# Another order for the first phase of a block-sparse gate kernel, with 21 instead of 13 opening matmuls that nobody reads

## The chip, the cores and the metric

The kernel runs on one core of one Trainium2 chip. The time is the device time of one execution, in microseconds (us). The core's engines run side by side, each through its own list of instructions in order: TensorE (PE, with its weight loads PEld), VectorE (DVE), ScalarE (ACT), GpSimd (POOL), and SyncE (SP), which here issues most DMA transfers.

## The reference, cut to what matters

```python
xn = _layernorm(x, axis=-1)                                   # x is [2, 1024, 1024], f32
bm = mask.reshape(Nb, 32, Kb, 32).sum(axis=(1, 3)) > 0        # 32 x 32 blocks
w = (weight.reshape(Nb, 32, Kb, 32) * bm[:, None, :, None]).reshape(N, K)
s = einsum('bsk,nk->bsn', xn, w) + bias
q = einsum('bi,ki->bk', xn.mean(axis=1), Wq)
coeffs = softmax(einsum('bk,ek->be', q, lora_keys) / sqrt(128))
base = einsum('bsi,oi->bso', xn, W_org)
delta = einsum('be,bser,ero->bso', coeffs, einsum('bsi,eir->bser', xn, lora_down), lora_up)
out = x + s * silu(base + delta)
```

All of it is float32. The change touches only batch 0, the product s for the first 512 output columns, and the way to the coefficients.

## The kernel before, in words

Every operand of a product is kept as two parts in the reduced format float32r: hi, the rounded value, which ACT writes with a copy, and lo, what remains, which DVE (at a few places POOL) writes with a subtraction. One 128-row step of a product is three matmuls in one accumulator: hi by hi (L457), hi by lo (L460), lo by hi (L461). So each step needs the hi and lo of its piece of x (tile g0, "xgrp" in the trace) and of its piece of the masked weights (s0, "slot").

The first phase makes s for the 1024 rows of batch 0 and the first 512 columns. Rows come in tiles 0 to 7 of 128. For tiles 0 to 3 the columns are done in two quarters of 256: p0 to p3 (their steps are called by t0 to t3) and q0 to q3 (by u0 to u3). Tiles 4 to 7 do 512 columns at once (q4 to q7, by u4 to u7). t0(0, 4) means steps 0 to 3 of the eight. The accumulators share four PSUM buffers in the order in which they are opened (open_gemm); one is taken again when its result has been moved out (quarter_evac, tile_evac on DVE). The first buffer is for warm_up(n): n matmuls of 512 columns on ones, whose result nobody reads.

The row tiles 0 to 3 arrive untransposed. For each, x_stats (DVE, two halves), rstd_of (two small DVE operations and a power on POOL), shift_of (DVE) and x_norm_half (ACT, twice) normalise it; x_turn (four PE transposes per half, into one of two pairs of PSUM buffers) turns it; x_hi (ACT) and x_lo (DVE) split it. Tiles 4 to 7 are read transposed already (xprep: a DMA of xT into one of six buffers "xt", a subtraction of the means on DVE, the hi copy on ACT; xprep_lo). spread_means makes their row of means with four transposes on PE. The tiles are also normalised in rows and added up into acc (add_acc, 1024 columns each), from which halves, query, scores and soft make the coefficients; scale_up multiplies lora_up with them for the product that follows the phase, y_mul.

The mask: mask_sum sums 0/1 blocks (DVE or ACT), mask_spread and mask_apply_mm (eight small bf16 matmuls, L276) spread the block flags over the partitions into the PSUM tile mp, mask_apply_cp copies it to m_sb. w_mul multiplies weights with it, from mp on DVE and from m_sb on POOL, which does not read PSUM here; w_hi and w_lo split them, for a quarter q and rows k0 on.

The order on PE, DVE, ACT and POOL is the order in which the program calls these helpers, since the block is under manual_schedule with those four engines; the order of SP's transfers is chosen by the scheduler of the language. A queue never overtakes: an instruction that waits holds all behind it on its engine.

Of the kernel before, what the change touches and what calls it, by code (L numbers as in the profile page):

```python
# [22 lines left out]
NH = 512  # L23
# [1 line left out]
TPB = S // P  # L25
E_, R_, KQ = 8, 64, 128
EPS = 1e-5
NWARM = 13
NWARM2 = 12


@with_exitstack
def kernel(
# [118 lines left out]
    def rstd_of(t):  # L152

        mv = small.tile([P, 2], F32, name="mv", bufs=10)
        nc.vector.bn_aggr(mv, stat[t])
        ve = small.tile([P, 1], F32, name="ve", bufs=3)
        nc.vector.tensor_scalar(ve, mv[:, 1:2], EPS, None, ALU.add)
        nc.gpsimd.tensor_tensor(rstd[:, t : t + 1], ve, mhalf, ALU.pow)
        means[t] = mv[:, 0:1]

    def shift_of(t):

        mr = small.tile([P, 1], F32, name="mr", bufs=3)
        nc.vector.tensor_scalar(mr, means[t], rstd[:, t : t + 1], -1.0, ALU.mult, ALU.mult)
        stat[t] = mr
# [84 lines left out]
    def mask_sum(qr, c, mt, eng, part=0):  # L250

        if qr not in msum:
            msum[qr] = small.tile([P, 2, 2], F32, name="s2")
        o = msum[qr][:, part, c : c + 1]
        if eng is nc.scalar:
            nc.scalar.activation(mt.bitcast(F32), mt, AF.Copy, accum_out=o)
        else:
            nc.vector.tensor_reduce(o, mt, AX.X, ALU.add)  # L258
# [23 lines left out]
    def mask_apply_cp(qr, k0=0, k1=NKT, copy=nc.vector.tensor_copy):  # L282
        copy(m_sb[:, k0:k1, 8 * qr : 8 * (qr + 1)], spread[qr][:, k0:k1, :])
# [300 lines left out]
    def w_mul(q, k0, eng, n=2):  # L584

        v = wh[q][:, k0 : k0 + n, :].rearrange("p k (b i) -> p k b i", i=32)
        m = m_sb[:, k0 : k0 + n, 8 * q : 8 * (q + 1)] if eng is nc.gpsimd else spread[q][:, k0 : k0 + n, :]
        eng.tensor_tensor(v, v, m.unsqueeze(3).to_broadcast([P, n, 8, 32]), ALU.mult)
# [10 lines left out]
    def x_turn(i, h):  # L599
        turn((i, h), lambda k: xr[i][:, (4 * h + k) * P : (4 * h + k + 1) * P])  # L600

    def x_hi(i, h):
        nc.scalar.copy(g0[:, 4 * h : 4 * h + 4, 0, i * P : (i + 1) * P], turned[(i, h)])
# [7 lines left out]
    def x_stats(i, h):  # L611
        bn(i, xr[i], h)
# [31 lines left out]
    def x_norm_half(i, h):  # L644
        v = xr[i][:, h * NH : (h + 1) * NH]
        norm(i, v, v)
# [5 lines left out]
    with tc.manual_schedule(engines={mybir.EngineType.PE, mybir.EngineType.DVE, mybir.EngineType.Activation, mybir.EngineType.Pool}):  # L652
# [19 lines left out]
        def warm_up(n):  # L672
            for _ in range(n):
                nc.tensor.matmul(
                    warm, lhsT=ones_r, rhs=ones_r.unsqueeze(1).to_broadcast([P, 4, P]), start=True, stop=True
                )

        warm_up(NWARM)
        x_stats(0, 0)
        x_stats(0, 1)  # L680
        rstd_of(0)
# [1 line left out]
        x_norm_half(0, 0)  # L683
        x_norm_half(0, 1)
        x_turn(0, 0)
        x_turn(0, 1)
        warm_up(NWARM2)
        x_stats(1, 0)
        x_stats(1, 1)
        rstd_of(1)  # L690
        mask_sum(0, 0, mh[0][:, 0, :], nc.vector)
        x_hi(0, 0)
        mask_sum(0, 1, mh[0][:, 1, NH:], nc.scalar, 1)
        mask_sum(0, 1, mh[0][:, 1, :NH], nc.vector)
        mask_join(0)
        mask_spread(0)
        shift_of(1)
        mask_apply_mm(0)
        warm_up(4)
        x_hi(0, 1)  # L700
        mask_apply_cp(0, 0, 4, nc.scalar.copy)
        w_mul(0, 0, nc.vector, 1)
        w_mul(0, 1, nc.vector, 1)
        w_mul(0, 2, nc.gpsimd)
        w_hi(0, 0, 1)
        w_hi(0, 1, 1)
        x_lo(0, 0)
        x_norm_half(1, 0)
        w_hi(0, 2)
        w_lo(0, 0, nc.vector, 1)  # L710
        w_lo(0, 1, nc.vector, 1)
        p0, t0 = open_gemm(0, 0, s0, 0, NQ)
        p1, t1 = open_gemm(0, 1, s0, 0, NQ)

        keep_busy = lambda kt: warm_up((4, 1, 2, 0)[kt])
        t0(0, 1, keep_busy)
        x_turn(1, 0)
        t0(1, 2, keep_busy)
        x_hi(1, 0)
        mask_apply_cp(0, 4, 8, nc.scalar.copy)  # L720
        w_lo(0, 2)
        t0(2, 4, keep_busy)
        x_lo(1, 0)
        w_mul(0, 4, nc.vector)
        w_mul(0, 6, nc.gpsimd)
        x_norm_half(1, 1)
        w_hi(0, 4)
        t1(0, 3)
        x_turn(1, 1)
        x_lo(0, 1)  # L730
        w_hi(0, 6)
        w_lo(0, 4)
        x_hi(1, 1)
        t1(3, 4)
        t0(4, 6)
        w_lo(0, 6, nc.gpsimd)
        x_stats(2, 0)
        x_stats(2, 1)
        rstd_of(2)
        mask_sum(1, 0, mh[1][:, 0, :], nc.scalar)  # L740
        t0(6, 8)
        x_lo(1, 1)
        shift_of(2)
        x_norm_half(2, 0)
        x_norm_half(2, 1)
        x_stats(3, 0)
        x_stats(3, 1)
        rstd_of(3)
        add_acc(1, nc.gpsimd)
        t1(4, 7)  # L750
        x_turn(2, 0)
        t1(7, 8)
        x_hi(2, 0)
        x_turn(2, 1)
        x_lo(2, 0)
        shift_of(3)
        x_hi(2, 1)
        x_norm_half(3, 0)
        x_norm_half(3, 1)
        x_lo(2, 1)  # L760
        mask_sum(1, 1, mh[1][:, 1, :], nc.vector)
        mask_spread(1)
        p2, t2 = open_gemm(0, 2, s0, 0, NQ)
        t2(0, 4)
        x_turn(3, 0)
        x_hi(3, 0)
        t2(4, 5)
        mask_apply_mm(1)
        mask_apply_cp(1, copy=nc.scalar.copy)
        w_mul(1, 4, nc.gpsimd)  # L770
        w_mul(1, 6, nc.gpsimd)
        x_lo(3, 0)
        x_turn(3, 1)
        t2(5, 8)
        w_mul(1, 0, nc.vector)
        x_hi(3, 1)
        x_lo(3, 1)
        w_hi(1, 0)
        w_mul(1, 2, nc.vector)
        p3, t3 = open_gemm(0, 3, s0, 0, NQ)  # L780
        t3(0, 8)
        w_hi(1, 2)
        w_hi(1, 4)
        w_hi(1, 6)
        w_lo(1, 0)
        quarter_evac(0, 0, p0)
        w_lo(1, 2)
        mean_sum(6)
        mean_sum(7)
        w_lo(1, 4)  # L790
        w_lo(1, 6)
        quarter_evac(1, 0, p1)
        x_stats(4, 0)
        x_stats(4, 1)
        x_stats(5, 0)
        rstd_of(4)
        x_stats(5, 1)
        q0, u0 = open_gemm(0, 0, s0, NQ, NQ)
        u0(0, 8)
        shift_of(4)  # L800
        x_norm(4)
        rstd_of(5)
        mean_of(6)
        mean_of(7)
        q1, u1 = open_gemm(0, 1, s0, NQ, NQ)
        u1(0, 6)
        spread_means(0, 1)
        u1(6, 8)
        quarter_evac(2, 0, p2)
        xprep(0, 1, 0)  # L810
        xprep(0, 1, 1)
        shift_of(5)
        x_norm(5)
        xprep_lo(0, 1, 0)
        quarter_evac(3, 0, p3)
        q2, u2 = open_gemm(0, 2, s0, NQ, NQ)
        u2(0, 8)
        q3, u3 = open_gemm(0, 3, s0, NQ, NQ)
        u3(0, 8)
        for kt in range(2, 6):  # L820
            xprep(0, 1, kt)
            xprep_lo(0, 1, kt - 1, nc.gpsimd if kt == 4 else nc.vector)
            if kt == 3:
                quarter_evac(0, 1, q0)
            square_sum(6 + (kt - 2) // 2, kt % 2)
        xprep(0, 1, 6)
        xprep_lo(0, 1, 5, nc.gpsimd)
        xprep(0, 1, 7)
        rstd_from(6)
        rstd_from(7)  # L830
        xprep_lo(0, 1, 6)
        xprep_lo(0, 1, 7)
        quarter_evac(1, 1, q1)
        q4, u4 = open_gemm(0, 4, s0)
        u4(0, 8)
        shift_of(6)
        shift_of(7)
        x_norm(6)
        x_norm(7)
        for i in range(2, 6):  # L840
            add_acc(i, nc.vector)
        quarter_evac(2, 1, q2)
        add_acc(6, nc.vector)
        quarter_evac(3, 1, q3)
        for h in range(2):
            add_acc(7, nc.vector, h)
        halves, query, scores, soft = coeffs(0)
        halves()
        y00 = new_slot()
        q5, u5 = open_gemm(0, 5, s0)  # L850
        u5(0, 8)
        q6, u6 = open_gemm(0, 6, s0)
        u6(0, 4)
        query()
        tile_evac("s", 0, 0, 4, q4)
        y_prep(0, 0, 0)
        u6(4, 7)
        scores()
        tile_evac("s", 0, 0, 5, q5)
        soft()  # L860
        scale_up(0, 0)
        y_prep(0, 0, 1)
        u6(7, 8)
        tile_evac("s", 0, 0, 6, q6)
        q7, u7 = open_gemm(0, 7, s0)
        u7(0, 8)
        for k in range(NKT):
            y_mul(0, 0, k)
            if k == 0:
                tile_evac("s", 0, 0, 7, q7)  # L870
            y_sum(0, 0, k)
            if k + 2 < NKT:
                y_prep(0, 0, k + 2)
            y_hi(y00, 0, 0, k)
            y_lo(y00, 0, 0, k)
            if k == 1:
                act_stats(0)
# [684 lines left out]
```

## Time and profile before

| | us |
|---|---|
| median of 3 runs | 438.7 (438.32 to 438.96) |
| the profiled execution | 438.7 |
| its span in the trace | 437.0 |
| first matmul without a use | 1.12 |
| first x_turn | 7.30 |
| first product (L457) | 13.15 |
| end of the first quarter of tiles 0 to 3, start of u0 | 30.68 |
| start of u4 | 42.62 |
| start of y_mul | 65.60 |
| last matmul starts | 432.58 |
| TensorE clock granted | 1.00 |

The span runs from the first instruction to the last; the 1.7 us between it and the execution's time lie outside the trace. "Busy" is the share of the span in which an engine works; a matmul without a use counts as busy. The names in the trace are those of the tiles: "pt" is a transposed tile in PSUM, "xgrp" the split x, "slot" the split weights, "ramp" the raw weights and masks, "mp" the spread mask, "acc_ps" an accumulator. A profile line can name what ended an engine's idle time, after "<-".

### The profile page before, as it was taken

What the parts mean: (1) busy time and instruction counts of PE and PEld (TensorE: products, weight loads), DVE (VectorE), ACT (ScalarE), POOL (GpSimd) and SP (SyncE); (2) the same over time, 40 slices, a digit from 0 to 9 for tenths busy, and PEclk for the clock granted to TensorE, in tenths of its full rate; (3) what the DMA queues carried; (4) which work ended last, traced back from release to release, by engine and by line L of the source; (5) the groups of instructions that cost most, each with busy time, mean ns of one, the idle gap of its engine ahead of it and who ended that gap; (6) DMA issues with size and microseconds to landing.
All of it is one profiled execution on the core that took longest, in us unless ns stands there. A gap on an engine that the chain in (4) does not pass through costs nothing.

```text
span 437.0 us, 5766 instructions
## 1 busy us (share of the span) xinstructions
PE 429.5 (98%) x2029; PEld 357.8 (82%) x2029; DVE 305.0 (70%) x508; ACT 184.6 (42%) x312; POOL 79.0 (18%) x103
## 2 busy tenths in 40 slices
PE   7999999999999999999999999999999999999996
PEld 5899888888888888888888878888888888888885
DVE  5889977766527779878957779867647385275624
ACT  3787436354731222246332454466335233441510
POOL 4342210002220323133130330010020030002000
PEclk9999999999999999999999999999999999999999
DMA  7994706787896799984689788976282165228003
GB/s 271 414 355 162 218 26 221 237 249 225 250 309 170 252 264 309 314 307 144 179 213 307 242 246 226 347 239 197 68 220 70 48 145 147 93 53 210 27 1 121
DMA packets 44477, 88.48 MB, mean 202 GB/s; under 512 B 4624, under 2 KB 13088, under 8 KB 44448
## 3 DMA queue, kind: packets, MB, share of 16 engines
q1 hardware_dynamic: 28944, 64.77, 44.3%
q0 software_dynamic: 6624, 16.26, 16.0%
q10 hardware_dynamic: 8880, 7.08, 5.1%
q8 instruction: 16, 0.26, 0.3%
q14 instruction: 13, 0.11, 0.1%
HBM read 68.17 MB, written 19.93 MB: 202 GB/s over the span
## 4 chain that ended last, share of the span: by engine, by line
PE 95%; DVE 1%; DMA 1%; ACT 1%; issue 0%; POOL 0%; SPq 0%; DVEq 0%
PE acc_ps L1393 25%; PE acc_ps L461 13%; PE acc_ps L457 13%; PE acc_ps L460 13%; PE py L1393 10%; PE psv L1148 6%; PE psw L422 3%; PE psw L423 3%; PE psw L421 3%; PE psw L1148 2%; DMA raw<-in_x_dram 1%; PE pt L211 0%; DVE s L258 0%; ACT slot L591 0%; POOL slot L595 0%
## 5 line engine op out<-in xcount | busy, mean ns | idle before, releaser
L1393 PE MATMUL acc_ps<-xw,ow 128*128 128x512 f32 (+1 forms) x492 | 111.9, 384 | 0.0
L457 PE MATMUL acc_ps<-slot,xgrp 128*128 128x512 f32 (+1 forms) x288 | 106.5, 370 | 0.2 <-ACT slot L591 0.2
L1393 PEld LDWEIGHTS acc_ps<-xw,ow 128*128 128x128 f32 x492 | 90.8, 188 | 18.3
L461 PE MATMUL acc_ps<-slot,xgrp 128*128 128x512 f32 (+1 forms) x288 | 105.5, 366 | 0.2 <-DVE xgrp L607 0.2
L460 PE MATMUL acc_ps<-slot,xgrp 128*128 128x512 f32 (+1 forms) x288 | 105.4, 366 | 0.1
L461 PEld LDWEIGHTS acc_ps<-slot,xgrp 128*128 128x128 f32 x288 | 54.2, 188 | 9.6 <-DVE xgrp L607 0.6
L457 PEld LDWEIGHTS acc_ps<-slot,xgrp 128*128 128x128 f32 x288 | 54.3, 188 | 9.3 <-ACT slot L591 0.6
L460 PEld LDWEIGHTS acc_ps<-slot,xgrp 128*128 128x128 f32 x288 | 54.3, 188 | 8.9 <-POOL slot L595 0.3
L1393 PE MATMUL py<-xw,ow 128*128 128x512 f32 x192 | 46.3, 389 | 0.0
L1393 PEld LDWEIGHTS py<-xw,ow 128*128 128x128 f32 x192 | 36.0, 188 | 7.5
L1262 DVE TENSOR_TENSOR ow<-raw,ow 128x1024 fp32r<-128x1024 f32 (+1 forms) x32 | 34.6, 1087 | 9.2 <-ACT ow L1261 9.1
L1261 ACT CAST ow<-raw 128x1024 fp32r<-128x1024 f32 (+1 forms) x32 | 29.5, 940 | 2.5 <-DVE raw L1255 1.7
L1376 POOL DMA_DIRECT2D gate<-in_xT_dram x12 | 10.5, 913 | 94.0 <-DVE gate L1370 67.8
L509 POOL DMA_DIRECT2D stash<-in_x_dram x16 | 14.4, 901 | 66.9 <-DVE stash L506 66.9
L431 ACT CAST slot<-wo 128x512 fp32r<-128x512 f32 x16 | 9.9, 620 | 35.8 <-DVE wo L428 35.6
L421 PE MATMUL psw<-cut,dhi 128*128 128x512 f32 x64 | 24.9, 389 | 0.0
L422 PE MATMUL psw<-cut,dhi 128*128 128x512 f32 x64 | 24.9, 389 | 0.0
L423 PE MATMUL psw<-cut,dlo 128*128 128x512 f32 x64 | 24.9, 389 | 0.0
L1437 DVE TENSOR_TENSOR py<-py,s 128x512 f32<-128x512 f32 x8 | 5.6, 698 | 26.8 <-ACT s L1400 26.8
L1255 DVE TENSOR_TENSOR raw<-raw 128x512 f32<-128x512 f32 x32 | 21.3, 688 | 0.9 <-DMA raw<-yu 0.4
L1247 DVE TENSOR_TENSOR raw<-raw,m_sb 128x1024 f32<-128x1024 f32 x8 | 9.7, 1221 | 14.4 <-DMA raw<-in_wu_dram 14.4
L506 DVE TENSOR_TENSOR stash<-stash,mine 128x512 f32<-128x512 f32 x16 | 11.1, 692 | 10.8 <-ACT mine L482 10.6
(211 smaller groups left out, 604.0 us busy)
## 6 DMA issues: line engine op xcount, KB each, us to landing
wo<-in_worgT_dram SPq DMA_DIRECT2D x24, 256.0 KB, 4.1
raw<-in_x_dram SPq DMA_DIRECT2D x11, 512.0 KB, 4.8
ds<-in_down_dram SPq DMA_DIRECT2D x16, 256.0 KB, 3.2
stash<-in_x_dram POOLq DMA_DIRECT2D x16, 256.0 KB, 5.7
raw<-in_wu_dram SPq DMA_DIRECT2D x8, 512.0 KB, 5.7
raw<-yu SPq DMA_DIRECT2D x8, 512.0 KB, 3.8
out_dram<-stash ACTq DMA_DIRECT2D x14, 256.0 KB, 4.2
misc<-xv SPq DMA_DIRECT2D x12, 256.0 KB, 4.2
```

Source lines behind the costliest of these rows:

```text
L421: nc.tensor.matmul(ps, lhsT=dhi[:, c, :], rhs=u[c][:, 0, :], start=c == 0, stop=False)
L422: nc.tensor.matmul(ps, lhsT=dhi[:, c, :], rhs=u[c][:, 1, :], start=False, stop=False)
L423: nc.tensor.matmul(ps, lhsT=dlo[:, c, :], rhs=u[c][:, 0, :], start=False, stop=c == 3)
L457: nc.tensor.matmul(ps, lhsT=xs[:, kt, 0, cols], rhs=w[:, kt, 0, wc], start=kt == 0, stop=False)
L460: nc.tensor.matmul(ps, lhsT=xs[:, kt, 0, cols], rhs=w[:, kt, 1, wc], start=False, stop=False)
L461: nc.tensor.matmul(ps, lhsT=xs[:, kt, 1, cols], rhs=w[:, kt, 0, wc], start=False, stop=kt == NKT - 1)
L509: nc.gpsimd.dma_start(res, x[at], accum_op=ALU.add)
L1148: nc.tensor.matmul(ps, lhsT=w[:, a, wl, c, :], rhs=u[:, ul, :], start=start and c == 0 and n == 0, stop=c == 1 and n == 2, skip_group_chec ...
L1255: nc.vector.tensor_tensor(raw[:, o], raw[:, a], raw[:, b], op)
L1261: nc.scalar.copy(o[:, a:b, 0], raw[:, a:b])
L1262: nc.vector.tensor_tensor(o[:, a:b, 1], raw[:, a:b], o[:, a:b, 0].bitcast(F32), ALU.subtract)
L1393: nc.tensor.matmul(ps, lhsT=o[:, a, wl, j, :], rhs=xw[j][:, m, xl, cols], start=start and j == 0 and k == 0, stop=j == 3 and k == 2, skip_ ...
```

## The change

The helpers stay as they are. The calls of the first phase come in another order, PE's, DVE's, ACT's and POOL's lists with them. No call is added or taken away but those of warm_up: 21 instead of 13 at the start, 12 as before in the second place, 5 instead of 4 after the first mask products, and in the first steps of tile 0 one behind step 0 and three behind step 2 instead of four, one and two. The diff, cut in its second half:

```diff
-NWARM = 13
-NWARM2 = 12
+NWARM = 21
...
         warm_up(NWARM)
+        keep_busy = lambda kt: warm_up((1, 0, 3, 0)[kt])
+        halves, query, scores, soft = coeffs(0)
+
+        p0, t0 = open_gemm(0, 0, s0, 0, NQ)
+        p1, t1 = open_gemm(0, 1, s0, 0, NQ)
         x_stats(0, 0)
...
         x_turn(0, 0)
+        x_hi(0, 0)
         x_turn(0, 1)
-        warm_up(NWARM2)
+        warm_up(12)
+        p2, t2 = open_gemm(0, 2, s0, 0, NQ)
         x_stats(1, 0)
         x_stats(1, 1)
         rstd_of(1)
+        x_hi(0, 1)
+        mask_sum(0, 1, mh[0][:, 1, NH:], nc.scalar, 1)
         mask_sum(0, 0, mh[0][:, 0, :], nc.vector)
-        x_hi(0, 0)
-        mask_sum(0, 1, mh[0][:, 1, NH:], nc.scalar, 1)
+        shift_of(1)
+        x_norm_half(1, 0)
+        x_norm_half(1, 1)
         mask_sum(0, 1, mh[0][:, 1, :NH], nc.vector)
         mask_join(0)
         mask_spread(0)
-        shift_of(1)
         mask_apply_mm(0)
-        warm_up(4)
-        x_hi(0, 1)
         mask_apply_cp(0, 0, 4, nc.scalar.copy)
+        x_lo(0, 0)
+        mask_apply_cp(0, 4, 8, nc.scalar.copy)
+        warm_up(5)
         w_mul(0, 0, nc.vector, 1)
+        w_hi(0, 0, 1)
         w_mul(0, 1, nc.vector, 1)
+        w_mul(0, 4, nc.vector)
+        w_hi(0, 1, 1)
+        x_turn(1, 0)
+        w_lo(0, 0, nc.vector, 1)
+        t0(0, 1, keep_busy)
+        w_lo(0, 1, nc.vector, 1)
+        x_stats(2, 0)
         w_mul(0, 2, nc.gpsimd)
...
-        p0, t0 = open_gemm(0, 0, s0, 0, NQ)
-        p1, t1 = open_gemm(0, 1, s0, 0, NQ)
-
-        keep_busy = lambda kt: warm_up((4, 1, 2, 0)[kt])
-        t0(0, 1, keep_busy)
-        x_turn(1, 0)
-        t0(1, 2, keep_busy)
         x_hi(1, 0)
-        mask_apply_cp(0, 4, 8, nc.scalar.copy)
         w_lo(0, 2)
+        w_mul(0, 6, nc.gpsimd)
+        t0(1, 2)
+        x_turn(1, 1)
+        x_stats(2, 1)
+        w_hi(0, 6)
+        w_lo(0, 6, nc.gpsimd)
         t0(2, 4, keep_busy)
+        x_hi(1, 1)
         x_lo(1, 0)
...
+        t1(0, 3)
+        t1(3, 4)
+        rstd_of(2)
         w_hi(0, 4)
+        w_lo(0, 4)
         x_lo(0, 1)
+        mask_sum(1, 0, mh[1][:, 0, :], nc.scalar)
+        q0, u0 = open_gemm(0, 0, s0, NQ, NQ)
         t0(4, 6)
         t0(6, 8)
         shift_of(2)
         x_norm_half(2, 0)
         x_norm_half(2, 1)
+        x_turn(2, 0)
+        x_hi(2, 0)
+        x_lo(1, 1)
+        t1(4, 7)
         x_stats(3, 0)
         x_stats(3, 1)
         rstd_of(3)
+        x_turn(2, 1)
+        x_hi(2, 1)
         t1(7, 8)
         x_lo(2, 0)
+        t2(0, 4)
         shift_of(3)
         x_norm_half(3, 0)
         x_norm_half(3, 1)
         mask_sum(1, 1, mh[1][:, 1, :], nc.vector)
         mask_spread(1)
         mask_apply_mm(1)
         mask_apply_cp(1, copy=nc.scalar.copy)
+        quarter_evac(0, 0, p0)
+        x_turn(3, 0)
+        x_turn(3, 1)
+        x_hi(3, 0)
+        x_lo(2, 1)
+        t2(4, 5)
+        w_mul(1, 2, nc.vector)
+        w_mul(1, 0, nc.vector)
+        x_lo(3, 0)
+        x_stats(4, 0)
+        x_hi(3, 1)
+        t2(5, 8)
...
+        w_mul(1, 6, nc.gpsimd)
+        quarter_evac(1, 0, p1)
+        w_hi(1, 2)
+        w_lo(1, 2)
+        mean_sum(7)
+        w_lo(1, 0)
+        mean_of(7)
+        x_stats(5, 0)
+        q1, u1 = open_gemm(0, 1, s0, NQ, NQ)
+        add_acc(1, nc.gpsimd)
+        w_mul(1, 4, nc.gpsimd)
+        w_hi(1, 4)
+        w_lo(1, 4)
+        w_hi(1, 6)
+        w_lo(1, 6)
+        quarter_evac(2, 0, p2)
+        u1(0, 6)
...
+        u0(0, 8)
...
         shift_of(4)
         spread_means(0, 1)
         xprep(0, 1, 0)
         xprep(0, 1, 1)
+        xprep(0, 1, 2)
+        quarter_evac(0, 1, q0)
+        u1(6, 8)
+        xprep_lo(0, 1, 1, nc.vector)
+        xprep_lo(0, 1, 0)
+        xprep(0, 1, 3)
+        xprep_lo(0, 1, 3, nc.gpsimd)
+        xprep_lo(0, 1, 2, nc.vector)
...
+        u3(0, 8)
...
+        u2(0, 8)
...
+        u6(0, 4)
...
         u4(0, 8)
+        u5(0, 8)
+        add_acc(7, nc.vector, 1)
         halves()
         query()
-        tile_evac("s", 0, 0, 4, q4)
         y_prep(0, 0, 0)
         u6(4, 7)
         scores()
-        tile_evac("s", 0, 0, 5, q5)
         soft()
-        scale_up(0, 0)
-        y_prep(0, 0, 1)
+        tile_evac("s", 0, 0, 4, q4)
         u6(7, 8)
         tile_evac("s", 0, 0, 6, q6)
         q7, u7 = open_gemm(0, 7, s0)
         u7(0, 8)
+        scale_up(0, 0)
+        y_prep(0, 0, 1)
+        tile_evac("s", 0, 0, 5, q5)
+        y00 = new_slot()
```

Between spread_means and u5 the other xprep, xprep_lo, shift_of, x_norm and add_acc calls are mixed with the evictions; add_acc runs in the order 2, 3, 5, 6, 4, 7, and the norms of tiles 4 to 7 in the order 4, 7, 5, 6. The rest of the kernel, from y_mul on, is the same.

More of the change, by code (lines that the diff above doesn't have):

```diff
@@ L696 @@
         mask_spread(0)
-        shift_of(1)
         mask_apply_mm(0)
-        warm_up(4)
-        x_hi(0, 1)
         mask_apply_cp(0, 0, 4, nc.scalar.copy)
+        x_lo(0, 0)
+        mask_apply_cp(0, 4, 8, nc.scalar.copy)
+        warm_up(5)
         w_mul(0, 0, nc.vector, 1)
+        w_hi(0, 0, 1)
         w_mul(0, 1, nc.vector, 1)
+        w_mul(0, 4, nc.vector)
[5 more added lines that the diff above has]
+        x_stats(2, 0)
         w_mul(0, 2, nc.gpsimd)
[L705 to L708, printed above, removed]
         w_hi(0, 2)
-        w_lo(0, 0, nc.vector, 1)
-        w_lo(0, 1, nc.vector, 1)
-        p0, t0 = open_gemm(0, 0, s0, 0, NQ)
-        p1, t1 = open_gemm(0, 1, s0, 0, NQ)
-        keep_busy = lambda kt: warm_up((4, 1, 2, 0)[kt])
-        t0(0, 1, keep_busy)
-        x_turn(1, 0)
-        t0(1, 2, keep_busy)
         x_hi(1, 0)
-        mask_apply_cp(0, 4, 8, nc.scalar.copy)
         w_lo(0, 2)
+        w_mul(0, 6, nc.gpsimd)
[4 more added lines that the diff above has]
+        w_lo(0, 6, nc.gpsimd)
         t0(2, 4, keep_busy)
+        x_hi(1, 1)
         x_lo(1, 0)
-        w_mul(0, 4, nc.vector)
-        w_mul(0, 6, nc.gpsimd)
-        x_norm_half(1, 1)
+        t1(0, 3)
+        t1(3, 4)
+        rstd_of(2)
         w_hi(0, 4)
-        t1(0, 3)
-        x_turn(1, 1)
+        w_lo(0, 4)
         x_lo(0, 1)
[L731 to L734, printed above, removed]
+        mask_sum(1, 0, mh[1][:, 0, :], nc.scalar)
+        q0, u0 = open_gemm(0, 0, s0, NQ, NQ)
         t0(4, 6)
[L736 to L740, printed above, removed]
         t0(6, 8)
-        x_lo(1, 1)
         shift_of(2)
@@ L748 @@
         rstd_of(3)
-        add_acc(1, nc.gpsimd)
-        t1(4, 7)
-        x_turn(2, 0)
+        x_turn(2, 1)
+        x_hi(2, 1)
         t1(7, 8)
-        x_hi(2, 0)
-        x_turn(2, 1)
         x_lo(2, 0)
+        t2(0, 4)
         shift_of(3)
-        x_hi(2, 1)
         x_norm_half(3, 0)
         x_norm_half(3, 1)
-        x_lo(2, 1)
         mask_sum(1, 1, mh[1][:, 1, :], nc.vector)
         mask_spread(1)
-        p2, t2 = open_gemm(0, 2, s0, 0, NQ)
-        t2(0, 4)
-        x_turn(3, 0)
@@ L766 @@
-        x_hi(3, 0)
-        t2(4, 5)
         mask_apply_mm(1)
         mask_apply_cp(1, copy=nc.scalar.copy)
-        w_mul(1, 4, nc.gpsimd)
[L771 to L782, printed above, removed]
+        quarter_evac(0, 0, p0)
+        x_turn(3, 0)
+        x_turn(3, 1)
@@ new lines @@
+        x_hi(3, 0)
[7 more added lines that the diff above has]
+        t2(5, 8)
+        p3, t3 = open_gemm(0, 3, s0, 0, NQ)
+        w_hi(1, 0)
+        x_lo(3, 1)
+        t3(0, 8)
+        w_mul(1, 6, nc.gpsimd)
[7 more added lines that the diff above has]
+        q1, u1 = open_gemm(0, 1, s0, NQ, NQ)
@@ L783 @@
+        add_acc(1, nc.gpsimd)
+        w_mul(1, 4, nc.gpsimd)
         w_hi(1, 4)
+        w_lo(1, 4)
         w_hi(1, 6)
-        w_lo(1, 0)
-        quarter_evac(0, 0, p0)
-        w_lo(1, 2)
+        w_lo(1, 6)
+        quarter_evac(2, 0, p2)
+        u1(0, 6)
         mean_sum(6)
[L789 to L793, printed above, removed]
+        mean_of(6)
+        square_sum(6, 0)
         x_stats(4, 1)
-        x_stats(5, 0)
+        square_sum(6, 1)
@@ L796 @@
+        quarter_evac(3, 0, p3)
         rstd_of(4)
+        square_sum(7, 0)
+        square_sum(7, 1)
+        u0(0, 8)
         x_stats(5, 1)
-        q0, u0 = open_gemm(0, 0, s0, NQ, NQ)
-        u0(0, 8)
+        rstd_of(5)
+        q3, u3 = open_gemm(0, 3, s0, NQ, NQ)
         shift_of(4)
[L801 to L806, printed above, removed]
         spread_means(0, 1)
-        u1(6, 8)
-        quarter_evac(2, 0, p2)
@@ L810 @@
         xprep(0, 1, 0)
         xprep(0, 1, 1)
-        shift_of(5)
-        x_norm(5)
[L814 to L825, printed above, removed]
@@ L826 @@
-        xprep(0, 1, 6)
-        xprep_lo(0, 1, 5, nc.gpsimd)
[L828 to L833, printed above, removed]
+        xprep(0, 1, 2)
[6 more added lines that the diff above has]
+        xprep_lo(0, 1, 2, nc.vector)
+        q2, u2 = open_gemm(0, 2, s0, NQ, NQ)
@@ new lines @@
+        q6, u6 = open_gemm(0, 6, s0)
+        u3(0, 8)
+        quarter_evac(3, 1, q3)
+        xprep(0, 1, 4)
+        shift_of(5)
+        xprep(0, 1, 5)
+        x_norm(4)
+        rstd_from(7)
+        xprep(0, 1, 6)
+        rstd_from(6)
+        quarter_evac(1, 1, q1)
+        xprep_lo(0, 1, 4, nc.vector)
+        add_acc(2, nc.vector)
+        shift_of(7)
+        q5, u5 = open_gemm(0, 5, s0)
+        x_norm(7)
+        xprep_lo(0, 1, 6)
+        u2(0, 8)
+        quarter_evac(2, 1, q2)
@@ L834 @@
+        xprep(0, 1, 7)
+        xprep_lo(0, 1, 7)
+        u6(0, 4)
+        x_norm(5)
+        shift_of(6)
+        add_acc(3, nc.vector)
+        add_acc(5, nc.vector)
+        x_norm(6)
+        add_acc(6, nc.vector)
+        add_acc(4, nc.vector)
+        add_acc(7, nc.vector, 0)
+        xprep_lo(0, 1, 5, nc.gpsimd)
         q4, u4 = open_gemm(0, 4, s0)
         u4(0, 8)
[L836 to L847, printed above, removed]
-        halves()
[L849 to L853, printed above, removed]
+        u5(0, 8)
+        add_acc(7, nc.vector, 1)
+        halves()
         query()
-        tile_evac("s", 0, 0, 4, q4)
         y_prep(0, 0, 0)
```

## The prediction

> **What bounds the kernel now.** I read the page's shares first, then its chain of waits, then the busy time by stretches, and last the timelines of PE, DVE, ACT and POOL up to 66 us.
>
> ```profile
> PE 429.5 (98%) x2029; PEld 357.8 (82%) x2029; DVE 305.0 (70%) x508; ACT 184.6 (42%) x312; POOL 79.0 (18%) x103
> PE 95%; DVE 1%; DMA 1%; ACT 1%; issue 0%; POOL 0%; SPq 0%; DVEq 0%
> ```
>
> PE is the bound. The page cannot say how much of its busy time is useful, because matmuls without a use count as busy. The stretches show where it is not dense (window, its length, then busy time and instructions of PE, PEld, DVE, ACT, POOL, the clock, DMA share, GB/s):
>
> ```profile
> 0.00:13.15 13.15, 10.09 (x45) 7.35 (x45) 8.10 (x23) 5.22 (x10) 5.24 (x11) 1.00 0.82 297
> 16.75:25.21 8.46, 8.14 (x62) 7.25 (x61) 7.58 (x17) 6.66 (x11) 4.62 (x5) 1.00 1.03 408
> 42.70:65.98 23.28, 23.28 (x105) 19.27 (x104) 20.31 (x42) 9.93 (x18) 4.65 (x5) 1.00 0.40 124
> ```
>
> From 42.6 us to the last matmul at 432.9 I find steps between matmul starts that are over 0.26 us in only 8 places, 0.75 us above the rest together. So a microsecond that PE is ahead at 42.6 us is one at the end, if nothing behind PE stops it. The first product starts at 13.15; before it PE can only wait. What the change can win lies between 13 and 31 us. PE's timeline there has the marks (start, length, idle before and releaser):
>
> ```profile
> 19.34 0.28 PE L457 MATMUL acc_ps<-slot,xgrp 128*128 128x256 f32 x1
> 19.68 0.39 PE L460 MATMUL acc_ps<-slot,xgrp 128*128 128x256 f32 x1
> ...
> 21.55 0.28 PE L461 MATMUL acc_ps<-slot,xgrp 128*128 128x256 f32 x1
> 21.87 0.66 PE L211 MATMUL pt<-ident,raw 128*128 128x128 f32 x4
> ...
> 23.42 0.28 PE L460 MATMUL acc_ps<-slot,xgrp 128*128 128x256 f32 x1
> 23.93 0.39 PE L461 MATMUL acc_ps<-slot,xgrp 128*128 128x256 f32 x1 [0.22 <-DVE xgrp L607]
> ```
>
> A dense step of a 256-column matmul is 0.12. Here steps are 0.34, 0.32 and 0.51. PE waits for w_lo(0,6) on POOL, for x_norm(2) on ACT (the list of waits has "PEld pt L211 <- ACT raw L168: 0.2"), for x_lo(2,0) on DVE. DVE has holes too, 2.4 us of them between 12 and 27 (0.53, 0.43, 0.41, 0.59, 0.48):
>
> ```profile
> 12.24 0.75 DVE L588 TENSOR_TENSOR ramp<-ramp,mp 128x256 f32<-128x256 f32 x2 [0.53 <-ACT m_sb L283]
> 14.69 0.69 DVE L595 TENSOR_TENSOR slot<-ramp,slot 128x512 fp32r<-128x512 f32 x1 [0.43 <-ACT slot L591]
> 15.79 0.69 DVE L607 TENSOR_TENSOR xgrp<-pt,xgrp 128x512 fp32r<-128x512 f32 x1 [0.41 <-ACT xgrp L603]
> ```
>
> The first line tells more: w_mul reads mp, not m_sb, and still starts 0.03 after ACT's copy of mp into m_sb (12.02 + 0.19). I take it that readers of one PSUM tile go one after the other.
>
> **How I walk the new order.** Each engine's list is followed by hand with steps of this trace: DVE 0.60 for 512 columns, 0.34 for 256, 1.2 for 1024, 0.16 to 0.24 for a small one that waits for the last; ACT cast 0.52 to 0.61, half a norm 0.72 (last one 0.81), 1024 columns 1.05 to 1.24; POOL w_mul 1.05, w_lo 1.29, add_acc 2.40, pow 0.55; PE 0.12 per 256-column product, 0.23 per warm matmul, 0.44 per four transposes; 0.035 from an engine to the next, 0.08 to POOL. SP's first 22 us (x, mask, weights, bias) issue the same transfers; they are held by earlier landings, so they land as now (x2 14.06, x3 17.9, x7 26.8).
>
> **To the first product.** The 21 warm matmuls: the first 7 start 0.43 apart (to 4.22), the rest 0.23, so they end at 4.22 + 14 x 0.2325 = 7.47. Now PE idles from 5.77 to 7.30, and that hides all but 0.17; x_turn(0,1) waits for its norm until 8.01 either way. Cost 0. Without this cover 8 matmuls cost 1.9. On DVE shift_of(1) moves ahead of the second mask sum: spread ends 11.71 instead of 11.59 (+0.12). On ACT both halves of norm(1) now stand ahead of the mask copies: mask sum to 10.96, norms 10.87 to 12.39, copies at 12.30 and 12.39, done 12.58 (now one copy, done 12.21). DVE fills its hole with x_lo(0,0) and starts w_mul at 12.62 (+0.37). w_hi 13.07 to 13.47. On PE: mask products 11.77, five warm to 13.20, x_turn(1,0) now ahead of the product, which starts at 13.56 (+0.40, but 0.44 of transposes is done).
>
> **The first four steps of tile 0.** DVE runs w_mul(0,4) before w_lo(0,0), so that one ends at 14.30, and the second product starts at 14.34; now it starts at 14.30 with four warm matmuls in between. The remaining warm are 3 in both orders. t0(0,4) with both transposes of tile 1 ends at 16.89. Now the same work without x_turn(1,1) ends at 16.75. **Lead 0.30** (0.44 - 0.14).
>
> **16.9 to 29.** x_lo(1,0) ends 17.04, just ahead of its product at 17.13; t1(0,4) ends 18.33; w_lo(0,4) is done 17.96, x_lo(0,1) 18.56 (needed 18.57). w_lo(0,6) is on POOL at 15.40 to 16.69 instead of 18.34 to 19.63, so the stall at 19.68 is gone: t0(4,8) ends 19.82 (now 20.38). norm(2) is 18.72 to 20.24, so x_turn(2,0) goes at 19.82, x_turn(2,1) at 21.34 without a wait; x_lo(2,0) is done 21.76, and t2(0,4) runs 22.13 to 23.57 (now to 25.21). **Lead 1.65.** What is late next is DVE. After mask_sum(1,1) (21.80 to 23.01) the second mask products are ready at 23.27, norm(3) ends 23.99, both transposes of tile 3 end 24.57, t2 26.09; x_lo(3,0) is done 26.08 (needed 26.33), x_lo(3,1) 27.28 (27.77). t3 ends at 28.97, now 30.68. **Lead 1.71.**
>
> **29 to the end.** u1 goes ahead of u0. POOL does w_mul(1,6), add_acc(1), then w_mul(1,4): 24.25, 25.30, 27.70 to 28.75; w_hi(1,4) 29.41, w_lo(1,4) 30.13; PE needs it at 30.53. ACT's mean_sum(7) waits for x7 (26.82) and delays nothing. spread_means has its last mean at 33.49 and runs at 34.01. DVE then idles 0.8 for it, with xprep(0) standing in front of an eviction. xprep 0 to 3 are split by 40.7, u6(0,4) needs them from 40.91 (now the next tile starts 42.62). The seventh and eighth xt transfers need the buffers of xprep_lo(0) and (1), free at 38.1 and 37.5 (now 38.3 and 39.9); with the 2.98 of the seventh it lands 41.2, and xprep(6) stands at 41.1. add_acc ends at 53.4 (now 55.15), halves at 54.8; the query's last product needs them at 55.26, so **DVE has 0.4 to spare**. The softmax ends near 61.1 (now 63.16), because two evictions moved behind it; scale_up's last split 65.0, needed 66.2. ds, wo and us move with their buffers, and new_slot moves with no instruction of its own; y_mul starts 63.9 instead of 65.6. Behind it the order is unchanged.
>
> **Sum** against the profiled execution (438.7, its span 437.0 plus 1.7): first product and transposes +0.04 less 0.44, warm and restarts +0.10, stalls 16.75 to 25.2 less 1.35, the rest less 0.06: **-1.7 us, 437.0**. The median of the runs shown is 438.7 as well. About 0.2% is what a measurement here can tell from no change.
>
> **A rule that speaks against the 21.** The trace has 7 slow steps, then the clock is full. The Trainium skill, "TensorE: Matmul & The Clock Gate", section "The HAM clock gate", says the slow stretch is a time of about 3.4 us, in windows that run free of the kernel's start, so the number of cold matmuls changes by run (6, 11 or 14 there). By the rule, and that is an estimate, a run with 14 cold ones would end the 21 at about 8.8. No run here shows that yet.
>
> From the trace alone I bound the 21 so: not below 0, since the clock reads 1.00 throughout already; at most all of them slow, 21 x 0.427 = 8.97, ending 10.1. They delay the mask products only if they end past 8.1. I take 0, the row itself.
>
> **Rivals.**
> 1. *DVE becomes the bound.* PE's margins to DVE are 0.01 to 0.5 at nine places; in my walk DVE has two holes only. For it: DVE is busy 20.3 of 23.3 in 42.7 to 65.98. Against: every step is from this trace. If DVE runs 1 us behind my walk, PE loses what is over 0.4 or so: 437.2 to 438.5, middle 437.8.
> 2. *POOL makes it slower.* add_acc(1), 2.40, now stands ahead of w_mul(1,4), which today starts at 26.73. u1 stops at its fifth step if w_mul(1,4) is over 0.4 late, and DVE stops at w_lo(1,4) with all evictions behind it; each further us costs one. The time is slower than before by over 0.2% from 0.4 + 1.7 + 0.9 = 3.0 late: 439.6 and more. For it: POOL's spans are rough. Against: POOL's add took 2.40 here with DVE busy beside it.
> 3. *The clock rises late*, near 10 instead of 4.2: the 21 end at 10.1, slow transposes add 0.9, the mask products come 2.9 late: 439.9; half as late, 437.5 to 438.5.
> 4. *It does not do what it says at the end*: the lead meets a transfer later on that does not move, 438.7. Against: PE's only waits behind 66 us are two of 0.1; transfers follow buffers that come free earlier.
>
> **Numbers.** Forecast 0.60 (436.3 to 437.7), DVE 0.20, POOL 0.08, clock 0.04, lost later 0.08. Faster: 0.60 + half of DVE 0.10 + 0.01 = 0.71. Same: 0.10 + 0.08 + 0.02 = 0.20. Slower: 0.08 + 0.01 = 0.09. The range goes from 436.3 (lead 2.4: the 0.75 of small steps gone too) to 438.5, the end of the DVE case.
>
> **What would show it.** First product near 13.55, behind x_turn(1,0); second near 14.34; no step above 0.26 between 17 and 24 except beside transposes; t2's first four steps over at 23.6; u1 at 29.0 with no wait for w_lo(1,4); next tile after the quarters at 40.9; y_mul at 63.9. Wrong would be a wait of PE for DVE at 17.1, 18.6 or 55.3, a POOL add over 2.8, or warm matmuls that end past 8.1.

## The result, and the profile after

The changed kernel takes 440.52 us (median of 6 runs, 439.93 to 441.22) against 438.79 (438.32 to 439.25) of the kernel before beside it: ratio 1.0036, 95% interval 1.0021 to 1.0050. It is slower by about 1.6 us, and the forecast was 1.7 faster. The profiled execution took 440.62, its span is 438.9. Line numbers are one lower than before: w_lo is L594, x_lo L606, w_mul L587, add_acc L649, xprep_lo L237.

The page first:

```profile
PE 431.8 (98%) x2035; PEld 359.7 (82%) x2035; DVE 308.9 (70%) x508; ACT 184.1 (42%) x312; POOL 79.6 (18%) x103
```

DVE runs the same 508 instructions and is busy 3.9 us longer (308.9 after 305.0). Nothing was added to it, so some of its operations take longer. That is the line to stop at. The stretches, as before, say where PE is not dense:

```profile
0.00:13.15 13.15, 12.03 (x51) 9.67 (x52) 7.80 (x21) 6.18 (x11) 4.40 (x11) 1.00 0.81 297
13.15:16.75 3.60, 2.96 (x20) 2.41 (x20) 3.59 (x7) 2.26 (x5) 2.82 (x3) 1.00 1.03 416
30.68:42.70 12.02, 11.57 (x97) 11.37 (x96) 11.07 (x27) 7.90 (x16) 2.12 (x4) 1.00 0.45 159
42.70:65.98 23.28, 22.88 (x105) 18.34 (x104) 19.66 (x40) 9.75 (x13) 4.95 (x5) 1.00 0.39 133
```

Between 13.15 and 16.75 DVE is busy all but 0.01 us, with 7 instructions in that stretch. In the kernel before it was busy for 2.76 us with 6:

```profile
13.15:16.75 3.60, 3.60 (x23) 3.28 (x24) 2.76 (x6) 2.90 (x6) 1.01 (x2) 1.00 1.03 414
```

PE's timeline of the changed kernel around the first products:

```profile
1.12 7.87 PE L673 MATMUL warm<-ones_r 128*128 128x512 f32 x21 [1.12 <-DVE ones_r L97]
8.83 1.03 PE L210 MATMUL pt<-ident,acc 128*128 128x128 f32 x8
...
12.46 0.36 PE L275 MATMUL mp<-r,misc 128*128 128x8 bf16 x8
...
14.27 0.36 PE L456 MATMUL acc_ps<-slot,xgrp 128*128 128x256 f32 x1
14.47 0.40 PE L673 MATMUL warm<-ones_r 128*128 128x512 f32 x1
15.51 0.39 PE L459 MATMUL acc_ps<-slot,xgrp 128*128 128x256 f32 x1 [0.64 <-DVE slot L594]
```

Two things differ from the forecast. The 21 warm matmuls do not end at 7.47: 14 of them start 0.43 apart instead of 7 (the full clock comes at 7.1 us, not 4.1; the clock column of the stretches reads 1.00 all the same, because the trace's record of the clock begins only then, so it is the spacing that shows it). So x_turn starts at 8.83 and the mask products at 12.46 instead of 11.77. And the second product waits for w_lo(0,0) until 15.51. What DVE and POOL do there (start, length):

```profile
14.43 1.36 DVE L594 TENSOR_TENSOR slot<-ramp,slot 128x256 fp32r<-128x256 f32 x2
15.71 0.68 DVE L149 BATCH_NORM_STATS2 st<-raw 128x6 f32<-128x512 f32 x1
16.32 1.48 DVE L594 TENSOR_TENSOR slot<-ramp,slot 128x512 fp32r<-128x512 f32 x1
```

```profile
13.12 2.06 POOL L587 TENSOR_TENSOR ramp<-ramp,m_sb 128x512 f32<-128x512 f32 x2 [3.34 <-ACT m_sb L282]
15.95 1.29 POOL L594 TENSOR_TENSOR slot<-ramp,slot 128x512 fp32r<-128x512 f32 x1 [0.78 <-ACT slot L590]
```

A w_lo of 512 columns took 0.69 before; two of 256 took 0.75, and an add_acc of 1024 took 1.21 to 1.23. From the kernel before:

```profile
13.51 0.75 DVE L595 TENSOR_TENSOR slot<-ramp,slot 128x256 fp32r<-128x256 f32 x2
...
52.41 1.21 DVE L650 TENSOR_TENSOR acc<-acc,xlate 128x1024 f32<-128x1024 f32 x1
```

In the changed kernel the two kinds of w_lo take 1.48 and 1.36. Each began while POOL was at work, and ended shortly after POOL did: POOL's second w_mul ends at 15.17 and the first w_lo at 15.46; POOL's w_lo ends at 17.25 and DVE's at 17.79. The same picture comes twice more: w_lo(1,0), the second of the two in the first line below, beside POOL's w_mul(1,4) (0.69 becomes 1.53), and add_acc(2) beside POOL's xprep_lo(5):

```profile
29.55 2.14 DVE L594 TENSOR_TENSOR slot<-ramp,slot 128x512 fp32r<-128x512 f32 x2
...
45.61 2.32 DVE L649 TENSOR_TENSOR acc<-acc,raw 128x1024 f32<-128x1024 f32 x1
```

```profile
29.64 1.51 POOL L587 TENSOR_TENSOR ramp<-ramp,m_sb 128x512 f32<-128x512 f32 x1
...
45.36 1.48 POOL L237 TENSOR_TENSOR xgrp<-xt,xgrp 128x512 fp32r<-128x512 f32 x1
```

The add_acc takes 2.32 instead of 1.22. But not every DVE operation beside POOL is stretched. While add_acc(1) ran on POOL from 27.28 to 29.69, DVE had these:

```profile
27.43 0.68 DVE L606 TENSOR_TENSOR xgrp<-pt,xgrp 128x512 fp32r<-128x512 f32 x1
28.03 0.69 DVE L149 BATCH_NORM_STATS2 st<-xlate 128x6 f32<-128x512 f32 x1
28.63 0.67 DVE L606 TENSOR_TENSOR xgrp<-pt,xgrp 128x512 fp32r<-128x512 f32 x1
```

x_lo reads one operand from PSUM (pt), the statistics read one tensor. The four that were stretched read two tensors from SBUF. In the profile of before, up to 66 us, no such operation stands beside a POOL operation on 512 columns or more for longer than 0.12 us: there POOL worked beside x_lo, w_mul from mp, xprep (which reads its means from PSUM), statistics and sums.

Further on, in the part that the change leaves alone, the kernel before has the same meeting. Two subtractions of 512 columns that read two SBUF tensors take 1.28 while POOL is idle, and 2.02 when POOL adds and subtracts SBUF tensors of 256 columns beside them:

```profile
198.81 1.28 DVE L1064 TENSOR_TENSOR cut<-raw,cut 128x512 fp32r<-128x512 f32 x2
...
203.14 2.02 DVE L1064 TENSOR_TENSOR cut<-raw,cut 128x512 fp32r<-128x512 f32 x2 [1.72 <-ACT cut L1063]
```

```profile
202.73 3.04 POOL L1094 TENSOR_TENSOR dr<-dr 128x256 f32<-128x256 f32 x3 [6.34 <-ACT dr L1092]
```

Such meetings between 203 and 260 us are in both kernels, and their number changes from run to run. Of DVE's 3.9 us the four new ones make 3.3; the rest lies there.

So there are two theories. PORT: a DVE operation with two SBUF inputs stands still while a POOL operation reads SBUF; four meetings stretch DVE by 0.61 + 0.79 + 0.84 + 1.10 = 3.34 us. CLOCK: the full clock comes late in some runs, and 21 warm matmuls, unlike 13, then hold up PE. The rival to both is that the new order itself makes PE wait.

### The profile page after: what moved, and what is told of

It is laid out like the page before. It is cut to its first block, busy times and chain, and to the rows that moved or that the text cites. A ratio compares the mean times of both kernels' runs of the same rounds, so it can differ in the third digit from the quotient of the medians.

```text
span 438.9 us, 5779 instructions
## 1 busy us (share of the span) xinstructions
PE 431.8 (98%) x2035; PEld 359.7 (82%) x2035; DVE 308.9 (70%) x508; ACT 184.1 (42%) x312; POOL 79.6 (18%) x103
## 4 chain that ended last, share of the span: by engine, by line
PE 87%; DMA 6%; DVE 5%; SPq 1%; issue 0%; ACT 0%; DVEq 0%; ACTq 0%
PE acc_ps L1401 25%; PE acc_ps L456 11%; PE acc_ps L459 11%; PE acc_ps L460 11%; PE py L1401 10%; PE psv L1156 6%; PE psw L422 3%; PE psw L420 3%; PE psw L421 3%; PE psw L1156 2%; DMA xlate<-in_x_dram 2%; DMA ramp<-in_wr_dram 2%; DVE acc L649 2%; DMA xt<-in_xT_dram 1%; DVE xt L230 1%; DVE xgrp L237 1%
```

## The experiments

Ratios are against runs of the kernel before on the same chip, which had medians of 438.8 to 439.2.

| kernel | median us | ratio, 95% interval |
|---|---|---|
| changed, 13 warm (after_13) | 440.27 | 1.0031, 1.0020 to 1.0042 |
| before, 21 warm (before_21) | 439.07 | 1.0013, 0.9999 to 1.0027 |
| changed without the four meetings, 21 warm (n21) | 437.41 | 0.9967, 0.9956 to 0.9978 |
| the same, 13 warm (n13) | 437.01 | 0.9961, 0.9948 to 0.9973 |
| after_13 without the first two meetings (s_q0) | 438.67 | 0.9990, 0.9977 to 1.0003 |
| after_13 without the third (s_w14) | 439.60 | 1.0022, 1.0011 to 1.0033 |
| after_13 without the fourth (s_lo5) | 439.39 | 1.0009, 0.9993 to 1.0026 |
| all work, calls moved apart, 13 warm (fix13) | 437.32 | 0.9965, 0.9952 to 0.9978 |
| before, with two POOL additions (probe_add) | 440.11 | 1.0025, 1.0013 to 1.0038 |
| before, with five POOL fills (probe_set) | 438.91 | 1.0001, 0.9982 to 1.0020 |
| fix13, x_turn(1,1) earlier (fix13b) | 437.75 | 0.9962, 0.9949 to 0.9975 |
| fix13b, 21 warm (fix21b) | 437.98 | 0.9980, 0.9965 to 0.9995 |

### The clock alone

```diff
-NWARM = 21
+NWARM = 13
```

> The changed kernel with 13 opening matmuls instead of 21. Two theories for the loss. CLOCK: the full clock came at 7.0 us instead of 4.2, the 21 ended at 8.83 and pushed the first product by 0.7 us. PORT: operations of DVE that read two SBUF tensors stand still while a POOL operation runs; four such meetings stretch DVE by 3.3 us and PE by some 2.9. If both hold, this kernel gains what the clock cost and keeps the rest: 439.8. If the clock were all of the loss against the forecast: 437.0. If only the port counts: 440.5. The first transposes should start at 7.3 again, and the first w_lo of tile 0 should still be stretched until POOL's w_mul(0,6) ends.

```diff
-NWARM = 13
+NWARM = 21
```

> The kernel before with 21 opening matmuls instead of 13, nothing else. CLOCK: if the full clock comes at 7.0 as in the profile of the changed kernel, the 21 end at 8.8, the mask products come at 12.4 instead of 11.64, and the time is 439.2 to 439.6; if it comes at 4.2, 438.8. PORT alone: 438.8, no change.

Taking the 8 back brings the changed kernel from 440.52 to 440.27, less than the 0.7 expected, and their intervals overlap. In its profile the mask products start at 11.65 again, 0.81 earlier, yet the loss stays: the clock is not the main cause. In the kernel before, 21 put the mask products at 11.96 instead of 11.64 (11 slow matmuls in that profile), and the time up by 0.13%, with an interval that just takes in no change.

### The four meetings taken away

What remains unchanged: all work of DVE and PE. What POOL leaves out is in the expectation; the last line of the diff is bookkeeping of the program, no instruction.

```diff
-        w_mul(0, 6, nc.gpsimd)
...
-        w_lo(0, 6, nc.gpsimd)
+        nc.gpsimd.memset(s0[:, 6:8, 1, :NQ].bitcast(F32), 0.0)
...
-        w_mul(1, 4, nc.gpsimd)
...
-        xprep_lo(0, 1, 5, nc.gpsimd)
+        nc.gpsimd.memset(group(0, 1)[:, 5, 1, :].bitcast(F32), 0.0)
+        staged.pop(("x", 1, 5))
```

> The changed kernel with 21 opening matmuls, without the POOL work that meets two-tensor operations of DVE: w_mul for steps 6 and 7 of the first quarter and 4 and 5 of the second is left out, and the lo parts of weight steps 6 and 7 (first quarter) and of x step 5 (tiles 4 to 7) are zeros that POOL writes instead of a difference. All of DVE's and PE's work is as in the changed kernel. PORT: every two-SBUF operation on DVE is back at its length of before (0.42 and 0.69), and the time falls by 2.5 to 3, to 437.5 to 438.0. If instead the new order itself makes PE wait: 440 or more.

> The same with 13 opening matmuls. CLOCK and PORT together: 437.0, the forecast, since what the forecast left out is then left out on the chip. If there is a third cause: more than 438.

437.41 and 437.01: the loss is gone, and the time is about the forecast's 437.0. That n13 meets it to the tenth is luck: the forecast was for 21 warm matmuls and all of POOL's work, and n13 is 2.00 us ahead of before at the last matmul, where the forecast had 1.71. DVE's list in n13 at the same place, with a fill on POOL in the first of its rows (13.35 to 13.87):

```profile
13.65 0.76 DVE L594 TENSOR_TENSOR slot<-ramp,slot 128x256 fp32r<-128x256 f32 x2
14.32 0.69 DVE L149 BATCH_NORM_STATS2 st<-raw 128x6 f32<-128x512 f32 x1
14.93 0.68 DVE L594 TENSOR_TENSOR slot<-ramp,slot 128x512 fp32r<-128x512 f32 x1
```

Without this work of POOL the order is a good one; "the new order makes PE wait" falls. The two kernels also take away every wait for what POOL would have written. The probes in the kernel before and fix13, further down, keep the two apart.

### One meeting at a time

Each has 13 warm matmuls and one of the three groups of edits above: the first three lines (s_q0), the w_mul(1, 4) line (s_w14), the last three (s_lo5).

> The changed kernel with 13 opening matmuls (440.27), without POOL's w_mul for weight steps 6 and 7 of the first quarter (left out) and with zeros written by POOL for their lo part; the other two meetings stay. PORT: the two stretched w_lo of the first quarter (0.61 and 0.77 us of DVE) are short again, PE gains 1.4: 438.9. If a single meeting made all the loss, this is either 437.0 or 440.3.

> The same base, only POOL's w_mul for weight steps 4 and 5 of the second quarter left out. PORT: w_lo(1,0) is 0.69 instead of 1.53, PE does not stop in the first steps of u1 (0.6 now): 439.7. Against PORT: no change, 440.3.

> The same base, only the lo part of x step 5 (tiles 4 to 7) as zeros written by POOL. PORT: add_acc(2) is 1.22 instead of 2.32, and the query's matmuls come 1.1 earlier: 439.2. Against PORT: no change, 440.3.

From 1.0031 the ratio falls by 0.0041, 0.0009 and 0.0022: 1.8, 0.4 and 1.0 us of 438.8. They add up to 3.2; all four together (1.0031 to 0.9961) are 3.1. The prices add within the intervals, so no single group carries the loss. The 0.4 of s_w14 alone is not clear of noise: its interval and that of after_13 overlap for the most part. In s_lo5 the addition on DVE is back to its length:

```profile
44.73 1.22 DVE L649 TENSOR_TENSOR acc<-acc,raw 128x1024 f32<-128x1024 f32 x1
```

### The port in the kernel before

The additions follow w_mul(1, 6, nc.gpsimd); the second kernel has five memset of spare_t in their place.

```diff
+        spare_t = stage_l.tile([P, NH], F32, name="junk", tag="g", bufs=1)
+        for _ in range(2):
+            nc.gpsimd.tensor_tensor(spare_t, xr[2][:, :NH], xr[3][:, :NH], ALU.add)
```

> The kernel before, with two additions on POOL behind w_mul(1,6) that read two SBUF pieces of 512 columns and write a tile that nobody reads. Nothing waits for them. PORT: they stand beside DVE's w_lo(1,0) and w_lo(1,2); these two, 0.69 each now, take about 1.7 each, DVE is 2 us late from there on, and PE meets that in u0 and at the query: 440.2 to 440.8. If only waits that the program writes count: 438.8, as before.

> The same with five fills on POOL in place of the two additions, some 2.6 us as well, which write the same tile but read no SBUF. PORT as the stretched rows show it (a fill beside w_lo did not stretch it in the kernel without the four meetings): 438.8, w_lo stays 0.69. If any work on POOL at that time is what costs: as much as the additions.

This takes the changed order out of the question. No instruction waits for the additions, and they cost 1.1 us (0.25%), a little less than expected; the fills cost nothing that can be seen. DVE beside the additions (POOL at them from 28.50 to 31.49):

```profile
28.63 1.72 DVE L595 TENSOR_TENSOR slot<-ramp,slot 128x512 fp32r<-128x512 f32 x1
30.27 0.41 DVE L473 TENSOR_TENSOR stash<-acc_ps,bias_bc 128x256 f32<-128x256 f32 x1
30.60 2.64 DVE L595 TENSOR_TENSOR slot<-ramp,slot 128x512 fp32r<-128x512 f32 x3
```

And beside the fills (28.74 to 31.60):

```profile
28.89 0.68 DVE L595 TENSOR_TENSOR slot<-ramp,slot 128x512 fp32r<-128x512 f32 x1
29.50 0.42 DVE L473 TENSOR_TENSOR stash<-acc_ps,bias_bc 128x256 f32<-128x256 f32 x1
29.83 1.89 DVE L595 TENSOR_TENSOR slot<-ramp,slot 128x512 fp32r<-128x512 f32 x3
```

1.72 against 0.68 with about the same time of POOL work beside it: an addition that reads SBUF stops DVE, a fill that only writes does not. The eviction between them reads PSUM and is not stretched.

### A version without the meetings that does all the work

```diff
         w_mul(0, 4, nc.vector)
         w_hi(0, 1, 1)
+        x_lo(0, 1)
...
-        x_stats(2, 0)
         w_mul(0, 2, nc.gpsimd)
         w_hi(0, 2)
         x_hi(1, 0)
         w_lo(0, 2)
+        x_stats(2, 0)
...
         rstd_of(2)
+        add_acc(1, nc.gpsimd)
...
-        x_lo(0, 1)
...
         w_mul(1, 6, nc.gpsimd)
+        w_mul(1, 4, nc.gpsimd)
...
-        add_acc(1, nc.gpsimd)
-        w_mul(1, 4, nc.gpsimd)
...
         x_norm(4)
+        xprep_lo(0, 1, 5, nc.gpsimd)
...
         quarter_evac(1, 1, q1)
+        xprep(0, 1, 7)
         xprep_lo(0, 1, 4, nc.vector)
...
-        xprep(0, 1, 7)
...
-        xprep_lo(0, 1, 5, nc.gpsimd)
```

> All work done, 13 opening matmuls, calls moved so that POOL's operations stand beside operations of DVE that read PSUM or one SBUF tensor: x_lo(0,1) ahead of the first w_lo, w_lo(0,2) ahead of x_stats(2,0), add_acc(1) behind rstd_of(2), w_mul(1,4) right behind w_mul(1,6), xprep_lo(5) behind norm(4), xprep(7) ahead of xprep_lo(4). PORT: no operation of DVE is stretched by more than 0.2, and the kernel is faster than before: 437.3 to 437.9. If the order as such is bad, it stays above 438.8.

437.32, faster than the kernel before by 0.35%, with every operation in place. No DVE operation up to 62 us is stretched. Now it is POOL that waits a little where DVE came first:

```profile
12.57 2.06 POOL L587 TENSOR_TENSOR ramp<-ramp,m_sb 128x512 f32<-128x512 f32 x2 [2.49 <-ACT m_sb L282]
15.40 1.60 POOL L594 TENSOR_TENSOR slot<-ramp,slot 128x512 fp32r<-128x512 f32 x1 [0.77 <-ACT slot L590]
```

The 1.60 is 1.29 and 0.31, and 0.31 is what was left of DVE's w_lo(0,2) (it ends at 15.85), less 0.14. The last two kernels move x_turn(1, 1) up behind x_turn(1, 0) in fix13, with 13 and with 21 warm matmuls:

> The repaired order with 13 opening matmuls (437.32), with x_turn(1,1) moved up behind x_turn(1,0), into the 1.16 step in which PE waits for the first w_lo. It takes 0.44 out of the path: 436.9. If PE's later margins to DVE are used up: 437.3.

> The same with 21 opening matmuls. CLOCK: between nothing (full clock at 4.0) and 0.7 (at 7.1) over the kernel with 13: 436.9 to 437.6, on average 437.3.

The move gave nothing that can be told (0.9962 after 0.9965). The step in which PE waits for the first w_lo fell from 1.16 to 0.74 as meant, but x_lo(1,0) is then waited for at 17.48 in a step of 0.50, which fix13 did not have. y_mul starts at 64.37 instead of 64.52, while the mask products happened to be 0.22 earlier. With 21 the ratio is 0.9980: 0.8 us worse than with 13 (0.23 by the medians), at the upper end of what was expected, though that run's profile had 7 slow matmuls only, as the kernel before. A profile is one execution, the ratio is of several, so the two needn't agree.

## Why the prediction was wrong

The first table shows the walk against what ran. The column n13 is the kernel without the four meetings and with 13 warm matmuls.

| us from the span's start | before | the walk | after | n13 |
|---|---|---|---|---|
| mask products | 11.64 | 11.77 | 12.46 | 11.64 |
| first product | 13.16 | 13.56 | 14.27 | 13.44 |
| second product | 14.30 | 14.34 | 15.51 | 14.13 |
| spread_means on PE | 35.72 | 34.01 | 36.76 | 33.86 |
| y_mul | 65.60 | 63.9 | 67.75 | 63.78 |
| last matmul starts | 432.58 | | 434.49 | 430.58 |

- **The step that failed** is "How I walk the new order": "DVE 0.60 for 512 columns, 0.34 for 256, 1.2 for 1024", as if the length of an operation did not depend on what stands beside it on POOL. The order moved four operations that read two SBUF tensors beside POOL work. They measured 1.03 for 0.42, 1.48 for 0.69, 1.53 for 0.69 and 2.32 for 1.22, and cost 3.1 us together. The forecast's 437.0 and 3.1 make 440.1; the rest up to 440.52 is of the size of what the 21 warm matmuls cost. "Against: POOL's add took 2.40 here with DVE busy beside it" was read from a row whose DVE neighbours were x_lo twice, an operation on one column and a sum, which are just the kinds that are not stretched. "Against: every step is from this trace" has the same gap: the lengths were from the trace, but not from beside such POOL work.
- **What should have been weighed.** The row is probe_add's 1.72 beside probe_set's 0.68. One like it was there to be read ahead of the prediction: the 2.02 beside 1.28 in the kernel before, at 203 and 199 us. The Trainium skill, "SBUF — State Buffer", section "SBUF: two separate sides", states the rule: DVE and GpSimd share a pair of ports as an exclusive lock; a DVE operation with two SBUF inputs takes it against a GpSimd operation that reads SBUF, whichever starts first has it for the whole instruction, and the other one stands still. The rows of POOL operations on 256 columns or more agree, POOL's 1.60 and the fills too; POOL's powers on 1 and 8 columns do not (last section). It was the rule that spoke against this change, and the prediction weighed another one.
- **"The 21 warm matmuls ... Cost 0"** was too low in the changed kernel's profile, where the mask products came 0.7 later than in the walk. In the 14 profiles of this case 6 to 14 warm matmuls were slow, and the full clock came between 4.0 and 7.1 us, with the same first matmul at 1.12. The row I took was near the quick end, and "the clock reads 1.00 throughout already" is no bound, since that column does not show the slow stretch. By the ratios the 8 more matmuls cost 0.3 us between n13 and n21, 0.2 between after_13 and the changed kernel, 0.6 in the kernel before and 0.8 between fix13b and fix21b; by the medians it is 0.15 to 0.4. All four pairs have the same sign, but none is clear of noise by itself. The quoted rule (6, 11 or 14 cold ones, by run) was right about the spread; its time of about 3.4 us was not what ran here, where the slow stretch lasted 2.9 to 6.0 us from the first matmul.
- **"I take it that readers of one PSUM tile go one after the other"** held: w_mul started at 13.16, 0.03 after ACT's second copy. Whether the program's waits or the chip make it so was not tried.
- **Lead 0.30, 1.65, 1.71**: not in the changed kernel, but on n13's time scale they are there: spread_means 1.86 and y_mul 1.82 ahead of before.
- **"So a microsecond that PE is ahead ... is one at the end"** held both ways: at y_mul after is 2.15 late and 1.91 at the last matmul, n13 1.82 ahead and 2.00.
- **"DVE has 0.4 to spare"** was nearly so: in n13 the halves are done at 54.90, and PE takes the last at 55.08 without a wait. In the changed kernel it was spent: PE waits for halves at the query (0.17 and 0.23 idle, steps of 0.55 and 0.73), since add_acc came 4 us later than in the walk.
- Of the rivals, POOL was named at the right place, w_mul(1,4), with the wrong mechanism: the loss came not from add_acc running long (2.41, where over 2.8 would have been the sign), but from POOL stopping DVE. That this rival's 439.6 and more holds the measured time is luck. The rival "the clock rises late", the one with the lowest chance, happened in part (14 slow): the mask products came 0.7 later.

What stays open: the price of the 21 warm matmuls is known only as some 0.2 to 0.8 us, since the slow stretch changes by run.

## What to carry to other kernels

Before an order is walked with lengths from a profile, sort the operations of DVE by what they read: two SBUF tensors, or one of them from PSUM, or one tensor. The first kind should not stand beside a POOL operation that reads some 256 columns of SBUF or more; give POOL its work beside the other kinds. DVE's busy time at an equal number of instructions is a first sign (305.0 to 308.9 here), but no proof: it is 306.4 in before_21, whose DVE order is that of the kernel before. The lengths of operations of one form, beside POOL and away from it, are the proof. Matmuls without a use at the start can delay work that has a time to keep: their number is fixed, the slow stretch is not.

## What the runs showed of the hardware that was not expected

- The stop goes both ways. POOL's w_mul(1,4) took 1.50 instead of 1.05 in the changed kernel, having started 0.09 after DVE's w_lo(1,2), and a power on one column 0.93 instead of 0.55, having started at 19.37 beside a w_lo of DVE.
- A POOL fill of 512 columns (0.53 in probe_set) does not stop a two-tensor operation of DVE, and is not stopped by it.
- POOL's powers on 1 and 8 columns do not stop DVE either, though they read SBUF. While the one on 8 columns ran in the kernel before (194.35 to 196.39), a DVE subtraction of two SBUF tensors of 512 columns took its usual 0.69 (194.78 to 195.47).
- Beside a POOL operation on 512 columns, a stretched operation of DVE ended 0.28 (256 columns), 0.55 (512) and 1.08 us (1024) after POOL did, 0.14 less than its own length. I read it so that the operation has begun and its reading waits.
